# Matmuls of zeros in the planned pauses of TensorE, in a two-layer network on one core

## The chip, the core and the metric

The kernel runs on one core of a Trainium2 chip. The core has five engines that run their own instruction streams side by side: TensorE (PE in the profile; its weight loads are shown as PEld), VectorE (DVE), ScalarE (ACT), GpSimd (POOL) and SyncE (SP, which here only issues transfers). Each engine executes its instructions in the order of its stream, and waits on semaphores for the others. The metric is the device time of one execution in microseconds.

## The reference

The input is x, 8 images of 384 channels by 32 x 32 points (1024 tokens each). Layer 0 is a Mamba block that runs over the tokens forwards and backwards, beside a 3x3 depthwise convolution. Layer 1 is causal attention with 6 heads and a feed-forward part. The piece that matters here is the scan of layer 0, for each direction:

```python
delta = jax.nn.softplus(jnp.einsum('blr,dr->bld', dt, dt_proj_w) + dt_proj_b)
A = -jnp.exp(A_log)
deltaA = jnp.exp(delta[..., None] * A)
deltaBu = (delta * u)[..., None] * Bm[:, :, None, :]

def step(h, inp):
    dA, dBu, c = inp
    h = dA * h + dBu
    return (h, jnp.einsum('bdn,bn->bd', h, c))
...
y = ys.transpose(1, 0, 2) + u * D_param
y = y * silu(z)
return jnp.einsum('bld,od->blo', y, out_proj_w)
```

The state h has 16 components for each of 384 channels. The output y sums over these components, and in the kernel over both directions too.

## The kernel before

**Scans.** For every image, 96 groups are computed: each holds 8 channels x 16 state components on the 128 partitions and 1024 tokens along the free side, for one direction. The steps of a group (function `group`, within `scans`) are:

- SP loads delta, broadcast over the state components, into a tile dA; ACT takes the exponential with scale nA (L1007).
- PE spreads delta times u over the partitions with two matmuls by the 0/1 matrix dup (function `spread`; the profile calls its tile ring). The ring is 3 banks of PSUM; a group uses the middle bank and one of the two at the sides, so a spread into the middle bank has to wait until the scan before has read it.
- DVE multiplies both halves by B (L1035) and runs the scan over 1024 tokens (L1041), which reads two banks of the ring.
- POOL multiplies the result by C (L1045).

**Sums.** After every two groups PE adds them into the tile y with the 0/1 matrix sel (function `sums`). y is one bank of PSUM, [128, 512] in f32. Eight calls of `sums` (2 directions x GJ, GJ = 4) make one y: the first overwrites (start), the last ends the sum. Then DVE reads y (L983) and the next y takes over the same bank. There are 6 y for each image, 48 in all.

**Everything else.** Projections, convolutions, attention and feed-forward of the images around run in between, with four more banks of PSUM for their results. Nearly all matmuls are issued by the helper `mm` (L327), the transposes of attention by L1261. An f32 matmul appears as two MATMUL records and two weight loads.

**The order.** The program doesn't issue instructions as its loops run. Each step is entered as an `Op` with an engine, a cost in microseconds (functions act, dve, pool, pe, pair, quad at the top of the file), its reads, writes and due time. `Plan.run` plays the engines through with these costs: at each turn it takes the earliest operation that can start, with the waits for banks and transfers as it reckons them, and returns the operations sorted by their planned start. At the end of the kernel a loop emits them in that order, with `manual_schedule`, so that the order on each engine is the plan's, while the real waits are done by semaphores. A planned pause of PE is where the plan lets PE start an operation later than it ended the one before. The plan's pauses leave no instruction behind: on the chip PE simply waits for the semaphores of its next instruction.

Constants are made at the start of the kernel, among them ident, the 128 x 128 unit matrix in f32.

Of the kernel before, what the change touches and what calls it, by code (L numbers as in the profile page):

```python
# [9 lines left out]
F32 = mybir.dt.float32  # L10
# [7 lines left out]
P = 128  # L18
# [9 lines left out]
GJ = 4  # L28
# [37 lines left out]
class Val:  # L66


    __slots__ = ("kind", "shape", "dtype", "name", "t", "slot", "writes", "reads", "left", "end", "first")
# [4 lines left out]


class Op:
    __slots__ = ("engine", "cost", "fn", "vals", "allocs", "at", "waits", "users", "ready", "table", "done", "nbytes", "index", "after", "placed", "urgent")


def act(n):  # L80
# [24 lines left out]
class Plan:  # L105
# [63 lines left out]
    def run(self):  # L169

        engines = ("PE", "ACT", "DVE", "POOL", "SP")
        free = {e: 0.0 for e in engines}
        ready = {e: [] for e in engines}
        dma = 0.0
        table = None
        slots = {k: [(0.0, i) for i in range(n)] for k, n in self.slots.items()}

        queue = {k: [] for k in slots}
        for o in self.ops:
            for v in o.allocs:  # L180
                if v.kind != "psm":
                    queue[v.kind].append((o.at, o.index, v))
                    o.waits += 1
        for q in queue.values():
            q.sort(key=lambda a: a[:2])
            q.reverse()
        owner = {}
        for o in self.ops:
            for v in o.allocs:
                owner[id(v)] = o  # L190

        def release(o, t):
            o.ready = max(o.ready, t)
            o.waits -= 1
            if o.waits == 0:
                ready[o.engine].append(o)

        def hand_out(kind):
            while queue[kind] and slots[kind]:
                v = queue[kind].pop()[2]  # L200
                t, v.slot = heapq.heappop(slots[kind])
                release(owner[id(v)], t)

        for o in self.ops:
            if o.waits == 0:
                ready[o.engine].append(o)
        for kind in queue:
            hand_out(kind)
        order = []

        def bank_time(o):

            need = {}
            for v in o.allocs:
                if v.kind == "psm":
                    need[v.kind] = need.get(v.kind, 0) + 1
            t = 0.0
            for k, n in need.items():
                if len(slots[k]) < n:
                    return None  # L220
                t = max(t, sorted(slots[k])[n - 1][0])
            return t

        total = len(self.ops)
        while len(order) < total:
            best = None
            for e in engines:
                cand = []
                for o in ready[e]:
                    t = o.ready  # L230
                    if o.allocs:
                        tb = bank_time(o)
                        if tb is None:
                            continue
                        t = max(t, tb)
                    if e == "SP" and not o.urgent:
                        t = max(t, dma - self.BACKLOG)
                    cand.append((max(t, free[e]), o))
                if not cand:
                    continue  # L240
                t0 = min(c[0] for c in cand)

                pick, key = None, None
                for t, o in cand:
                    if t <= t0 + 0.05:
                        a = o.at - (self.STAY if e == "ACT" and o.table in (None, table) else 0.0)
                        k = (a, o.index)
                        if key is None or k < key:
                            pick, key, start = o, k, t
                if best is None or start < best[0]:  # L250
                    best = (start, e, pick)
            assert best is not None, "the slots do not suffice"
            start, e, o = best
            ready[e].remove(o)
            for v in o.allocs:
                if v.kind == "psm":
                    _, v.slot = heapq.heappop(slots[v.kind])
            cost = o.cost
            if e == "ACT" and o.table is not None and o.table != table:
                cost += self.SWITCH  # L260
                table = o.table
            free[e] = start + cost
            o.done = start + cost + self.LATENCY
            if e == "SP":
                dma = max(dma, start + cost) + o.nbytes / self.DMA_RATE
                o.done = dma + self.DMA_LATENCY + self.LANDING
            order.append((start, len(order), o))
            for u in o.after:
                release(u, start)
            for u in o.users:  # L270
                release(u, (o.done if u.engine != e or e == "SP" else free[e]) + (0.0 if u.urgent or u.engine == e else self.SLACK))
            for v in o.vals:
                v.left -= 1
                v.end = max(v.end, o.done)
                if v.left == 0 and v.kind is not None:
                    heapq.heappush(slots[v.kind], (v.end, v.slot))
                    if v.kind != "psm":
                        hand_out(v.kind)
        order.sort(key=lambda a: a[:2])
        return [o for _, _, o in order]  # L280
# [3 lines left out]
def conv_attn_hybrid_kernel(  # L284
# [20 lines left out]
    nc = tc.nc  # L305
    const = ctx.enter_context(tc.tile_pool(name="const", bufs=1))
# [4 lines left out]
    ident = const.tile([P, P], F32, name="ident")  # L311
# [14 lines left out]
    def mm(out_, lhsT, rhs, first=True, last=True):  # L326
        return nc.tensor.matmul(out_, lhsT=lhsT, rhs=rhs, start=first, stop=last)  # L327
# [1120 lines left out]
            forward(b, x2)  # L1448

    order = plan.run()  # L1450
    table = None
    with tc.manual_schedule():
        for o in order:
            for v in o.allocs:
                if v.kind in ("bs", "bm"):
                    continue
                p = pp if v.kind in ("psm", "y") else sb
                v.t = p.tile(v.shape, v.dtype, tag=f"{v.kind}_{v.slot}", name=v.name)
            if o.table is not None and o.table != table:
                table = o.table  # L1460
                nc.scalar.preload_act_table_set(table)  # L1461
            o.fn()


# [60 lines left out]
```

## Time and profile before

| What | Value |
|---|---|
| median of 3 runs | 4113.69 us (4110.54 to 4115.77) |
| the profiled execution, its own time | 4114.34 us |
| its span, from first to last instruction | 4112.4 us |
| mean granted clock of TensorE | 0.926 of full speed |
| scans on DVE (L1041) | 768, 2286 ns each, 1755.5 us |
| products by B on DVE (L1035) | 1536, 697 ns each, 1071.2 us |
| products by C on POOL (L1045) | 768, 2365 ns each, 1810.6 us |
| spreads on PE (ring) | 1536, 318.6 us busy |
| sums into y on PE | 3072 records, 533.5 us busy |
| idle of PE before a spread, until a scan ends | 339.0 us in 376 waits, at most 4.2 us |

In the profile, busy time is given for each engine, and also by 40 equal slices of the span, one digit for tenths of a slice. The row PEclk is the clock that TensorE was granted, in the same tenths. Matmuls are pipelined and their ends are modelled, so a busy PE isn't at its peak. The chain of waits follows the work that ended last back to what released it. A count such as x1536 is of instructions, and "128x512 f32" is partitions x elements.

### The profile page before, as it was taken

The page shows a single profiled execution, that of the slowest core. Times are in us where ns is not written, and L with a number is a line of the kernel's source. Part 1 is how long each engine was busy: PE and PEld are TensorE (multiplying, and loading weights), DVE is VectorE, ACT ScalarE, POOL GpSimd, SP SyncE. Part 2 cuts the span into 40 slices and gives each one's busy share as a digit, 9 for nine tenths or more (in the row PEclk, how much of TensorE's full clock was granted, in tenths as well). Part 3 has the DMA queues.
Part 4 walks back from the last instruction along what each step waited for, and adds up shares of the span by engine and source line. Part 5 has one row for each costly group of instructions (what it writes and reads, how often), then busy time and mean ns, then how long its engine had stood idle before and what let it go on. Part 6 is the DMA issues. An engine that isn't in the chain of part 4 may idle for free. (4 is left out here: it accounts for less than half of the span.)

```text
span 4112.4 us, 54637 instructions
## 1 busy us (share of the span) xinstructions
PE 3511.7 (85%) x17970; PEld 1407.7 (34%) x17970; DVE 3430.8 (83%) x3661; ACT 2815.4 (68%) x4547; POOL 3000.8 (73%) x2370
## 2 busy tenths in 40 slices
PE   6466658899998999898998899988999888898898
PEld 2111112443234422443234432444234432443363
DVE  2399989989989899888989899889998899999522
ACT  3766447775787758885778857786787766665364
POOL 1889786997589955997579965998479965775231
PEclk9687679899999999899999999999998899999999
DMA  7899897579976898669976798669975697559100
GB/s 243 233 258 275 254 263 203 156 227 256 265 207 181 233 265 242 189 207 240 271 211 196 218 260 248 197 199 246 253 230 174 177 255 203 141 161 228 48 9 35
DMA packets 302003, 858.96 MB, mean 209 GB/s; under 512 B 38312, under 2 KB 91576, under 8 KB 301720
## 3 DMA queue, kind: packets, MB, share of 16 engines
q1 hardware_dynamic: 301720, 855.47, 74.6%
q8 instruction: 143, 2.34, 0.2%
q14 instruction: 140, 1.15, 0.1%
HBM read 696.44 MB, written 160.68 MB: 208 GB/s over the span
## 5 line engine op out<-in xcount | busy, mean ns | idle before, releaser
L1045 POOL TENSOR_TENSOR dA<-dA,bc 128x1024 f32<-128x1024 f32 x768 | 1810.6, 2365 | 724.5 <-DVE dA L1041 638.7
L1041 DVE TENSOR_TENSOR_SCAN dA<-dA,ring 128x1024 f32<-128x1024 f32 x768 | 1755.5, 2286 | 91.4 <-ACT dA L1007 27.6
L1035 DVE TENSOR_TENSOR ring<-ring,bc 128x512 f32<-128x512 f32 x1536 | 1071.2, 697 | 286.1 <-PE ring L327 171.8
L1007 ACT ACTIVATE dA<-dA,nA 128x1024 f32<-128x1024 f32 x768 | 860.8, 1145 | 249.8 <-DMA dA<-ded 245.1
L327 PE MATMUL ring<-du,dup 32*128 32x512 bf16 x1536 | 318.6, 410 | 384.4 <-DVE dA L1041 339.0
L327 PE MATMUL y<-dA,sel 128*32 128x512 f32 x3072 | 533.5, 659 | 28.6 <-POOL dA L1045 26.2
L1208 ACT ACTIVATE p<-s,mx 128x512 f32<-128x512 f32 (+3 forms) x576 | 330.9, 581 | 99.7 <-DVE mx L1201 98.8
L1201 DVE TENSOR_REDUCE mx<-s 128x1 f32<-128x512 f32 (+3 forms) x576 | 286.0, 546 | 134.1 <-PE s L327 130.4
L1254 POOL TENSOR_SCALAR p<-p,den 128x512 f32<-128x512 f32 (+3 forms) x576 | 329.1, 590 | 79.0 <-issue 47.0
L327 PEld LDWEIGHTS <-dup 32*128 32x128 bf16 x1536 | 73.1, 92 | 887.1 <-DVE dA L1041 779.9
L1268 ACT COPY pT<-t 128x512 f32<-128x512 f32 (+3 forms) x576 | 258.1, 483 | 163.1 <-PE t L1261 156.2
L1261 PE MATMUL t<-ident,p 128*128 128x128 f32 x1728 | 298.1, 304 | 74.3 <-ACT pT L1268 26.2
L327 PE MATMUL s<-k,q 64*128 64x512 f32 (+3 forms) x1152 | 301.8, 571 | 20.6 <-ACT p L1208 19.1
L327 PE MATMUL pi<-xp,win 128*128 128x512 f32 x576 | 287.7, 621 | 3.5 <-DMA win<-in_in_wT 2.0
L1261 PEld LDWEIGHTS t<-ident,p 128*128 128x128 f32 x1728 | 206.1, 152 | 212.1 <-POOL p L1254 83.7
L1461 ACT ACT_TABLE_LOAD x210 | 269.4, 1283 | 4.5 <-PEq L1514 0.8
L327 PE MATMUL pc<-pT,v 128*64 128x128 f32 x3456 | 261.9, 294 | 10.1 <-ACT pT L1268 5.6
L327 PEld LDWEIGHTS pc<-pT,v 128*64 128x64 f32 x3456 | 204.4, 146 | 105.6 <-ACT pT L1268 38.6
L918 ACT CAST part<-u 128x1024 bf16<-128x1024 f32 x144 | 150.3, 1044 | 88.7 <-POOL u L926 49.1
L926 POOL TENSOR_TENSOR u<-u,part 128x1024 f32<-128x1024 f32 x96 | 205.0, 2135 | 5.6 <-ACT part L918 5.5
L327 PEld LDWEIGHTS y<-dA,sel 128*32 128x32 f32 x3072 | 82.3, 113 | 287.2 <-issue 137.9
L327 PEld LDWEIGHTS s<-k,q 64*128 64x128 f32 x1152 | 116.7, 197 | 144.4 <-ACT p L1208 64.4
(183 smaller groups left out, 4714.5 us busy)
## 6 DMA issues: line engine op xcount, KB each, us to landing
dA<-ded SPq DMA_DIRECT2D x768, 512.0 KB
ct<-urd SPq DMA_DIRECT2D x96, 513.5 KB
du<-dusd SPq DMA_DIRECT2D x96, 512.0 KB
xs<-xpd SPq DMA_DIRECT2D x96, 432.8 KB
dusd<-part SPq DMA_DIRECT2D x288, 128.0 KB
ded<-de SPq DMA_DIRECT2D x48, 512.0 KB
uz<-uzd SPq DMA_DIRECT2D x48, 512.0 KB
bc<-bcd SPq DMA_DIRECT2D x32, 512.0 KB
```

The lines of the kernel that those rows point to most:

```text
L327: return nc.tensor.matmul(out_, lhsT=lhsT, rhs=rhs, start=first, stop=last)
L926: "POOL", pool(L), lambda part=part: nc.gpsimd.tensor_sub(du.t, du.t, part.t), [part], [du]
L1007: "ACT", act(L) + 0.1, lambda: nc.scalar.activation(dA.t, dA.t, AF.Exp, scale=nA.t[:, g : g + 1]),
L1035: uses("DVE", nc.vector.tensor_mul(to, to, bc.t[:, 0, half(hf)]), [bank_of(v)])
L1041: i = nc.vector.tensor_tensor_scan(dA.t[:, rev], dA.t[:, rev], t[:, rev], 0.0, ALU.mult, ALU.add)
L1045: op("POOL", pool(L), lambda: nc.gpsimd.tensor_mul(dA.t, dA.t, bc.t[:, 1]), [(bc, 1)], [dA], at=at - PRODUCTS)
L1201: lambda sc=sc, g=g, w=k1 - k0, hh=hh: nc.vector.tensor_reduce(mx.t[:, g, hh : hh + 1], sc[hh].t[:, 0:w], AX.X, ALU.max, negate=True), [sc ...
L1208: nc.scalar.activation(ps[hh].t[:, k0:k1], sc[hh].t[:, 0 : k1 - k0], AF.Exp, bias=mx.t[:, g, hh : hh + 1], accum_out=den.t[:, g, hh : hh + 1],
L1254: nc.gpsimd.tensor_scalar(t, t, den.t[:, g, hh : hh + 1], 1.0, ALU.mult, ALU.mult)
L1261: nc.tensor.transpose(t.t[:, j * P - k0 : (j + 1) * P - k0], ps[hh].t[:, j * P : (j + 1) * P], ident)
L1268: nc.scalar.copy(pT[hh].t[:, k0 // P : k1 // P, :].rearrange("p j t -> p (j t)"), t.t[:, 0 : k1 - k0])
L1461: nc.scalar.preload_act_table_set(table)
```

## The change

After the plan has been made, the new code goes through the operations of PE in their order. Where the planned start of an operation lies more than 0.4 us after the planned end of PE's work so far, and a y has had at least one of its eight sums but not the last, it notes a number of pads for this operation: the pause less 0.2 us, divided by 0.25 us, rounded down. When the operations are emitted, so many matmuls of a 128 x 128 tile of zeros by ident are issued just before that operation. They are added onto the first 128 columns of the open y, without start and stop, so they add zero to it. The tile of zeros is written once, on POOL. The planner itself only stores each operation's start; costs, due times and order are untouched.

```diff
 class Op:
-    __slots__ = (..., "after", "placed", "urgent")
+    __slots__ = (..., "after", "placed", "urgent", "start")
...
+            o.start = start
             order.append((start, len(order), o))
...
     order = plan.run()
+
+    BUSY, REST = 0.25, 0.2
+    zeros = const.tile([P, P], F32, name="zeros")
+    nc.gpsimd.memset(zeros, 0.0)
+    at_work, parts_of, pads = 0.0, {}, {}
+    opened = None
+    for o in order:
+        if o.engine != "PE":
+            continue
+        pause = o.start - at_work
+        if opened is not None and pause > 2 * REST:
+            pads[id(o)] = (opened, int((pause - REST) / BUSY))
+        at_work = max(at_work, o.start + o.cost)
+        for v in o.vals:
+            if v.kind == "y":
+                parts_of[id(v)] = parts_of.get(id(v), 0) + 1
+                opened = v if parts_of[id(v)] < 2 * GJ else None
+
     table = None
     with tc.manual_schedule():
         for o in order:
...
+            if id(o) in pads:
+                y, k = pads[id(o)]
+                for _ in range(k):
+                    mm(y.t[:, 0:P], zeros, ident, False, False)
             o.fn()
```

## The prediction

> **What bounds the kernel now.** I read the page's engine totals and 40 slices first, then busy times by stretch, then waits, then the chain.
>
> ```profile
> PE 3511.7 (85%) x17970; PEld 1407.7 (34%) x17970; DVE 3430.8 (83%) x3661; ACT 2815.4 (68%) x4547; POOL 3000.8 (73%) x2370
> ...
> PE   6466658899998999898998899988999888898898
> DVE  2399989989989899888989899889998899999522
> ...
> POOL 1889786997589955997579965998479965775231
> PEclk9687679899999999899999999999998899999999
> ```
>
> PE, DVE and POOL share the bound. From slice 7 to slice 37 (617 to 3804 us, "the middle" below) PE is 91% and DVE 92% busy. From 206 to 617 us ("the head"; the scans of image 0 run, PE has little else) DVE alone sets the pace. After 3804 us ("the tail") there are no scans. How the pace looks where DVE sets it, from the chain of waits (start, length, what):
>
> ```profile
> 2906.39 2.30 DVE dA L1041
> 2910.39 2.30 DVE dA L1041
> 2914.39 2.30 DVE dA L1041
> ```
>
> One scan each 4.00 us: 2.29 of scan, two ring multiplies of 0.70, and 0.31 of handing over. So a DVE that waits for nothing still shows about 8% idle (0.31/4.00). In the attention stretches POOL is full as well (columns: stretch, length, busy us of PE, PEld, DVE, ACT and POOL with counts, clock, DMA share, GB/s):
>
> ```profile
> 3187.00:3290.00 103.00, 88.17 (x539) 44.50 (x533) 85.45 (x104) 76.20 (x163) 100.59 (x99) 0.88 0.61 177
> ```
>
> **The clock.** I asked for the busy times again in stretches of 3.413 us over the whole span. Nearly every stretch then shows a clock of 0.50 or 1.00, so it changes at these borders. One drop:
>
> ```profile
> 2211.82:2215.23 3.41, 2.95 (x20) 1.22 (x18) 3.20 (x3) 3.02 (x8) 3.35 (x3) 1.00 0.58 137
> 2215.23:2218.64 3.41, 1.57 (x8) 0.80 (x8) 3.31 (x8) 3.41 (x9) 3.31 (x3) 0.98 0.02 8
> 2218.64:2222.06 3.42, 0.86 (x4) 0.86 (x5) 3.42 (x6) 1.95 (x7) 3.42 (x6) 0.50 0.35 145
> 2222.06:2225.47 3.41, 3.41 (x19) 2.31 (x19) 2.25 (x3) 1.91 (x4) 3.27 (x5) 0.52 0.36 108
> 2225.47:2228.88 3.41, 3.16 (x39) 2.09 (x36) 3.09 (x6) 3.29 (x9) 2.62 (x5) 1.00 0.38 147
> ```
>
> PE is busy 46% of the second stretch; the next two run at half clock; a full stretch brings the clock back. In the middle all 19 warm stretches under 50% busy are followed by half clock, 8 of 27 at 50 to 60%, 11 of 131 at 60 to 80%, 1 of 673 above. There are 84 half-clock stretches there (287 us) in 39 episodes, 60 in the head (205 us), 8 in the tail.
>
> [...] The commonest kind (35 of some 78 us of idle in front of the drops) is the spread into the ring that waits for a scan:
>
> ```profile
> 1666.86 0.28 PE L327 MATMUL s<-neg,ident 128*128 128x128 bf16 x2
> 1668.47 0.39 PE L327 MATMUL ring<-du,dup 32*128 32x512 bf16 x2 [1.32 <-DVE dA L1041]
> ```
>
> **What the change adds.** Nothing is removed or moved: the planner's order is as before (the new field only stores a start). One memset on POOL at the start lies beside the first 100 us, in which POOL works 14. Then pads: a 128x128 f32 product of zeros each, ahead of a PE operation whose planned start leaves over 0.4 us of pause, while a y is between its first and eighth sum.
>
> Price of one pad. The nearest row is the v projection, the same shape and type; with its start and length and that of a 512-column f32 sum from the chain:
>
> ```profile
> 3964.32 5.36 PE pvv L327 x48
> ...
> 4055.64 5.15 PE pv_f L327 x12
> ```
>
> An f32 product is two MATMUL records (1152 pvv records for 576 products), so a pad is 5.36/24 = 0.223 us warm, about 0.446 at half clock; the plan allows 0.25. [...] I take the row, which is f32.
>
> Number of pads. The plan's pauses are no view of the profile, so I bound them by the real ones. PE gaps over 0.4 us: 68 in the head (143 us) and 322 in the middle (287 us); the rule of the diff, int((gap - 0.2)/0.25), makes 474 and 735 of them. y is open for about 7/8 of the time: 415 and 640. The plan counts 0.967 us for a 512-column f32 product where the trace has 5.15/6 = 0.86, so it sees less pause; against that it counts 1.07 for a sum into y where 533.5/384 = 1.39 are busy. I take 415 + 500, about 900 pads; ends 500 (few pauses planned) and 1500 (DVE's plan slower than I think). [...]
>
> What hides them: the very wait that the pause foresees. PE executes in order, so a pad costs only where PE reaches that place late. Behind it then stand the spread, the ring multiply, the scan and its POOL product. A pad runs 0.027 us shorter than allowed, 0.2 us and on average 0.12 of rounding stay free, and the plan's DVE has no handing over (3.69 us a scan against 4.00), so real waits at a scan should be longer than planned ones. If the cover is gone for all 500 pads of the middle: +111 us. If it holds: 0. I take one pad in eight uncovered, 14 us of PE, of which a fifth reaches DVE (it waits for PE in only part of the middle): +3 us.
>
> In the head a step leaves PE idle for 3.6 us in every 4.0 where it has nothing else:
>
> ```profile
> 238.93:242.34 3.41, 0.61 (x2) 0.10 (x2) 3.07 (x4) 1.15 (x1) 3.41 (x3) 0.50 0.78 265
> ```
>
> 13 pads are 2.9 us warm, inside the gap; the first such gap may meet the half clock (5.8 us) and hold DVE for 2.4 us, once or twice.
>
> What a steady clock is worth. Upper end: PE is busy 259 us in the middle's half-clock stretches; at full clock that work takes half, 130 us less, if PE alone were the path. Lower end: 0, if POOL and DVE cover all. The nearest rows are the waits of DVE in the middle (us, times, longest):
>
> ```profile
> DVE ring L1035 <- PE ring L327: 63.2, 70, 3.0
> DVE mx L1201 <- PE s L327: 38.5, 33, 4.2
> ```
>
> DVE's busy share is 0.847 in the half-clock stretches, 0.813 in the first stretch after each, 0.917 in the other warm ones. So the half clock costs DVE (0.917-0.847)x287 = 20 us and (0.917-0.813)x137 = 14 us, 34 together, a third of the 102 us of the two waits. The head adds (0.927-0.889)x205 = 8. I take three quarters of the 42 as prevented, because nearly all drops begin with y open, but those begun by a late POOL or DMA are foreseen only in part: -31 us. The tail has no open y: 0.
>
> Sum: 4114.3 (the profiled execution: 4112.4 of span and 2 around it) - 31 + 3 = 4086. It stands 0.6 us from the median of the runs, 4113.7, so 4086 against that too. What is late next is DVE with its 4.00 us a scan, and POOL in attention.
>
> **Rivals.**
> 1. *The pads take PE's room to catch up* (slower). PE's idle is also its slack after a late DMA or POOL. Filled with a fixed count, it no longer absorbs them, and pads run while a spread is due. The place is the ring spread in the attention stretches; the price 0.223 us a pad. It decides from 31/0.223 = 140 uncovered pads on the path. At half of the 500: +56 - 31, 4139. For it: the order is fixed and PE 91% busy. Against: the margins above.
> 2. *Hidden anyway* (no change). The drops lie mostly in attention, where POOL is at 97 to 99%; a faster PE waits for it. Then only the head's few us are left, 4108 to 4114. Against: the 63 and 38 us that DVE waits for PE.
> 3. *The pads don't do it* (no change): few planned pauses fall on the drops, or products of zeros don't count as work for the clock. No row shows zeros. 4114.
> 4. *PE is the path in the middle* (more). Three quarters of the 130 us are won: 4114 - 97 = 4017. For it: backlog from a half-clock episode lasts beyond the one stretch that I counted. Against: DVE is just as full.
>
> **How the numbers follow.** This kernel's runs lie within 0.13%, so 0.2% (8 us) is what can be told from no change: 4105.5 to 4122. Forecast (4065 to 4105) 0.53; rival 4 0.14; rivals 2 and 3 together 0.14; rival 1 0.19. Faster: 0.53 + 0.14 = 0.67; same 0.14; slower 0.19. The range takes the forecast's and both same-cases, reaches down over most of rival 4, and up to about its half-way mark in rival 1: 4030 to 4135.
>
> **What would show it.** Right: some 1800 more PE MATMUL records at y from zeros; the mean clock from 0.926 to about 0.96, the head's digits at 8 or 9; in the middle fewer than 30 half-clock stretches; PE's wait for scans down from 339 us to under 150; DVE's wait for PE below 63. Wrong: a clock that stays (rival 3), a clock that rises with the same span (2), DVE's wait for the spread above 63 us (1), or a span under 4050 (4).

## The result and the profile after

| | before | with the change |
|---|---|---|
| median of 20 runs each | 4116.65 us | 4110.17 us |
| ratio, 95% interval | | 0.9980 (0.9968 to 0.9992) |
| mean clock of TensorE in the profile | 0.926 | 0.964 |
| half-clock stretches (3.4 us) in the head / the middle | 60 / 84 | 10 / 37 |
| PE busy in the profile | 3511.7 us | 3650.7 us |

The change gains 0.2%, some 8 us, where 28 were forecast. The clock did what was expected of it as a mean: 0.96 was forecast. In the middle 37 half-clock stretches are left, where fewer than 30 were forecast. The page of the changed kernel, its totals and slices:

```profile
PE 3650.7 (89%) x20072; PEld 1623.8 (39%) x20072; DVE 3431.1 (83%) x3661; ACT 2815.7 (68%) x4547; POOL 3001.4 (73%) x2371
...
PE   6478889899998989889988989889998989998998
...
PEclk9699999999999999999999999999999999999899
...
L328 PE MATMUL ring<-du,dup 32*128 32x512 bf16 x1536 | 307.1, 393 | 307.7 <-DVE dA L1042 265.0 <-DMA du<-dusd 32.1 <-DVE den L1248 4.9
...
L328 PE MATMUL y<-ident,zeros 128*128 128x128 f32 x2102 | 296.2, 287 | 0.0
```

The head is slices 3 to 6: there the digits of PE went from 5 or 6 to 7 or 8, those of the clock from 6 to 8 up to 9. PE's idle before the spreads, until a scan ends, fell from 339 us only to 265.0; under 150 was named as the sign of being right. Most of the pads' time did not go into that wait. The last row is the pads: 2102 records, two to a pad, so 1051 pads (900 forecast), about 500 of them in the middle (500 forecast). DVE's waits for PE in the middle, the rows that answer to 63.2 and 38.5 before:

```profile
DVE ring L1036 <- PE ring L328: 48.0, 64, 2.4
DVE mx L1202 <- PE s L328: 32.1, 29, 4.2
```

They fell by 22 us. Yet the profiled execution before took 4112.4 us of span and this one 4113.8. Single runs scatter by more than the effect (4103 to 4126 with the change), so I took a second profile of each kernel:

> The kernel before once more, for a second profile. If the first was typical: 75 to 95 half-clock stretches in the middle, DVE waits 95 to 115 us for PE there, of which some 50 in or just after half clock.

> The changed kernel once more, for a second profile. If the first was typical: 30 to 45 half-clock stretches in the middle, DVE waits 75 to 95 us for PE there, of which under 25 in or just after half clock, and 50 to 65 where PE is warm and full.

The spans were 4122.8 and 4104.4. In the middle there were 89 and 40 half-clock stretches, DVE waited 111.1 and 79.9 us for PE, 57.2 and 25.3 of it in or just after half clock (the second a little over the 25 expected), and 51.7 with the change where PE was warm and full. Both first profiles were typical.

**A way to add up.** From the last read of y of image 0 to that of image 7, DVE has the same work in every kernel that keeps its work. I summed its idle gaps there, by what ended them (gaps between two instructions of one kind are left out). The time of this stretch less the idle is 3021 to 3026 us in all of these profiles, so what differs between kernels in this stretch is DVE's idle:

| profile | stretch, us | DVE idle | ended by PE | by ACT, POOL, DMA |
|---|---|---|---|---|
| before, two profiles | 3274.1, 3279.3 | 250.0, 256.5 | 109.2, 115.4 | 46.1, 46.5 |
| change, two profiles | 3277.6, 3267.4 | 253.7, 243.6 | 102.8, 98.8 | 56.1, 49.0 |

The rest of the idle, 94 to 96 us in each of the four, is short gaps between DVE's own instructions, and the change leaves it as it is. Means: DVE's idle falls by 4.6 us. Inside it:

- waits for PE that end in half clock or in the 3.4 us after it, in the middle: 51.5 and 57.2 before, 24.9 and 25.3 after, **-29 us**. This is the gain the change is after.
- waits for PE where it is warm and was over 90% busy in the 6 us before: 47.4 and 46.1 before, 53.5 and 51.7 after, **+6 us**. Those where it was warm but had been idle: -3. (With the limit at 95% these two are +2 and 0.)
- waits for PE between image 0 and 617 us: 0.7 and 0.8 before, 6.5 and 6.6 after, **+6 us**.
- waits for PE after 3804 us, the last 40 us of the scans: 3.0 and 3.8 before, 12.9 and 12.4 after, **+9 us**.
- waits for ACT, POOL and transfers: **+6 us**, with 7 between the two profiles of the change. Probably a DVE that is earlier meets the others sooner; that is not shown.

The head gives another -3 (image 0 ends at 569.6 and 572.2 before, 568.4 and 568.0 after). Together about -8, which is what was measured. With two profiles of each kernel, 10 us apart, the terms of 3 to 6 us are known only roughly, but for the +6 before 617 us: it is a single block of pads, the same in both profiles of the change. PE's order, and DVE's wait in that place:

```profile
605.06 7.63 PE L328 MATMUL y<-ident,zeros 128*128 128x128 f32 x66
612.63 0.39 PE L328 MATMUL ring<-du,dup 32*128 32x512 bf16 x2
```

```profile
DVE ring L1036 <- PE ring L328: 6.1, 1, 6.1
```

The plan has a pause of over 8 us there (33 pads at 0.25), and 33 pads were put into it. Before, PE waited 3.2 to 3.6 us for a scan ahead of the spreads around that time. The spread comes late and DVE stands for 6.1 us.

The +6 of the middle has no single place. What can make it, in the order of PE's work with the change (start, length, what, idle before and what ended it):

```profile
789.21 0.61 PE L328 MATMUL y<-ident,zeros 128*128 128x128 f32 x4
790.72 0.39 PE L328 MATMUL ring<-du,dup 32*128 32x512 bf16 x2 [0.90 <-DVE dA L1042]
791.03 1.16 PE L328 MATMUL y<-ident,zeros 128*128 128x128 f32 x8
792.12 1.06 PE L328 MATMUL y<-dA,sel 128*32 128x512 f32 x8
793.12 0.49 PE L328 MATMUL y<-ident,zeros 128*128 128x128 f32 x2
793.46 0.93 PE L1262 MATMUL t<-ident,p 128*128 128x128 f32 x4
```

The first two pads lie in a real wait: after them PE still waits 0.90 us for a scan. The next four and the one after do not: the sum and the transposes follow at once, so they were ready before the pads ended, and the pads made them late by up to their whole length. Counted over the middle, 371 of 498 pads are followed by work without any idle: 149 of them stand ahead of sums into y, 77 ahead of scores, 67 of transposes, and only 17 ahead of spreads. The plan lets these operations start later than they are ready on the chip. Which of its costs is too long there is not shown.

The +9 at the end of the scans is one place too, the same in both profiles of the change. PE's order and the busy times (PE, PEld, DVE, ACT, POOL, then the clock) there:

```profile
3819.10 1.65 PE L328 MATMUL y<-ident,zeros 128*128 128x128 f32 x6
3820.68 2.08 PE L328 MATMUL ph<-fy,w_fc 32*128 32x512 f32 x4
3822.68 1.94 PE L328 MATMUL y<-dA,sel 128*32 128x512 f32 x8
3824.55 0.61 PE L328 MATMUL ring<-du,dup 32*128 32x512 bf16 x2
```

```profile
3816.00:3820.00 4.00, 4.00 (x10) 2.07 (x11) 3.04 (x4) 1.78 (x3) 2.35 (x1) 0.50 0.00 0
3820.00:3824.00 4.00, 4.00 (x16) 1.16 (x15) 2.60 (x2) 1.09 (x2) 1.93 (x1) 0.50 0.00 0
3824.00:3828.00 4.00, 4.00 (x18) 0.81 (x14) 2.70 (x2) 0.00 (x0) 0.43 (x1) 0.50 0.00 0
```

PE is full and stays at half clock for 34 us. Three pads take 1.65 us there, where they took 0.94 at full clock just before, and the spread is due before it is issued: DVE waits 2.5 us for it. That the clock stayed at half through these 34 us, with PE full, is not what the prediction had assumed.

### The profile page after: what moved, and what is told of

Same layout as the page of the kernel before. It is cut to its first block, busy times and chain, and to the rows that moved or that the text cites. A ratio compares the mean times of both kernels' runs of the same rounds, so it can differ in the third digit from the quotient of the medians.

```text
span 4113.8 us, 58842 instructions
## 1 busy us (share of the span) xinstructions
PE 3650.7 (89%) x20072; PEld 1623.8 (39%) x20072; DVE 3431.1 (83%) x3661; ACT 2815.7 (68%) x4547; POOL 3001.4 (73%) x2371
## 5 line engine op out<-in xcount | busy, mean ns | idle before, releaser
L328 PE MATMUL ring<-du,dup 32*128 32x512 bf16 x1536 | 307.1, 393 | 307.7 <-DVE dA L1042 265.0
L328 PE MATMUL y<-dA,sel 128*32 128x512 f32 x3072 | 474.6, 619 | 13.0 <-POOL dA L1046 6.8
L1269 ACT COPY pT<-t 128x512 f32<-128x512 f32 (+3 forms) x576 | 256.5, 484 | 150.1 <-PE t L1262 143.3
L1262 PE MATMUL t<-ident,p 128*128 128x128 f32 x1728 | 283.4, 292 | 54.3 <-POOL p L1255 23.8
L328 PE MATMUL y<-ident,zeros 128*128 128x128 f32 x2102 | 296.2, 287 | 0.0
L328 PE MATMUL s<-k,q 64*128 64x512 f32 (+3 forms) x1152 | 278.2, 546 | 12.5 <-ACT p L1209 11.1
L328 PEld LDWEIGHTS y<-ident,zeros 128*128 128x128 f32 x2102 | 258.3, 195 | 69.8 <-issue 69.8
L1262 PEld LDWEIGHTS t<-ident,p 128*128 128x128 f32 x1728 | 195.2, 146 | 178.4 <-POOL p L1255 80.2
L328 PE MATMUL pc<-pT,v 128*64 128x128 f32 x3456 | 248.0, 284 | 4.7 <-ACT pT L1269 4.1
L328 PEld LDWEIGHTS pc<-pT,v 128*64 128x64 f32 x3456 | 192.6, 139 | 91.5 <-ACT pT L1269 35.4
```

The costliest lines, as they stand in the source:

```text
L1262: nc.tensor.transpose(t.t[:, j * P - k0 : (j + 1) * P - k0], ps[hh].t[:, j * P : (j + 1) * P], ident)
L1269: nc.scalar.copy(pT[hh].t[:, k0 // P : k1 // P, :].rearrange("p j t -> p (j t)"), t.t[:, 0 : k1 - k0])
```

## The experiments

Ratios are to the kernel before, with 95% intervals. "Half-clock stretches" and "waits" are those of the middle.

**e1, pads where PE was seen idle.** The pads' places and numbers come from the trace of before, ahead of spreads only:

```diff
-        pause = o.start - at_work
-        if opened is not None and pause > 2 * REST:
-            pads[id(o)] = (opened, int((pause - REST) / BUSY))
+        if any(v.kind in ("bs", "bm") for v in o.vals):
+            if opened is not None and nth in SEEN:
+                pads[id(o)] = (opened, SEEN[nth])
+            nth += 1
```

> Pads not where the plan has pauses but where the trace of before shows PE idle over 0.4 us ahead of a spread into the ring (259 gaps, 1023 pads by the same formula, those outside an open y skipped). Theory A (what was won is hidden: DVE's 4.00 us a scan and POOL set the end, PE does not): the clock rises to 0.95 or more, the time is as with the change, ratio 0.996 to 1.000. Theory B (the clock is worth some 30 us, and pads that run where PE is late give 20 us of it back): here nearly all pads lie in real idle, so the ratio is 0.991 to 0.995.

Measured 0.9988 (0.9977 to 1.0000), clock 0.951: both in theory A's ranges, and theory B's is missed. It is no proof of A, since the mean clock rose mostly in the head. Of some 290 pads in the middle 240 had idle left behind them, and the waits with PE warm and full were 50.5 us, between those before (47) and with the change (53). But 66 half-clock stretches remained there, with 41.6 us of waiting. Covered pads cost little, and these held the clock little too. Neither theory had that.

**e2, e3: PE lighter and heavier.**

```diff
 def sums(...):
+    if j == 1:
+        return
```

> The changed kernel without the sums of j = 1 (96 of 384 calls; a quarter of the terms of y is left out), which takes 474.6/384 = 1.24 us each, about 119 us, from PE, some 95 us of them in the middle. Theory A: at most 15 us of it reach the end, ratio 0.994 to 0.998. Theory B (PE on the path in the middle): 30 to 95 us reach it, ratio 0.975 to 0.991.

Measured 0.9983 (0.9970 to 0.9996), the same as with the change, just over theory A's range and far from theory B's. As a test of PE's place it fell short: half-clock stretches went up from 37 to 55, so that PE was busy only 46 us less in the middle, not 95. What was taken from PE's work came back with the clock (0.955 on average, against 0.964).

```diff
             o.fn()
+            for v in o.vals:
+                if o.engine == "PE" and v.kind == "y":
+                    sums_of[id(v)] = sums_of.get(id(v), 0) + 1
+                    for _ in range(2 if sums_of[id(v)] < 2 * GJ else 0):
+                        mm(v.t[:, 0:P], zeros, ident, False, False)
```

> The changed kernel with 2 more pads after each of the first seven sums of every y, whether PE has a pause or not: 672 more pads, 150 us of PE at 0.223 each, about 125 us in the middle. Theory A: PE's room takes it up, ratio up to 1.001. Theory B (uncovered pads cost about a quarter of their length): 30 us or more above the change, ratio 1.005 to 1.012.

Measured 1.0100 (1.0073 to 1.0127): 42 us above before, 50 above the change, for 672 more pads at an equal clock (33 half-clock stretches). That is a third of the pads' 150 us. DVE's waits for the spread answer directly (48.0 with the change):

```profile
DVE ring L1036 <- PE ring L328: 98.2, 113, 7.2
```

So pads that run where PE is late do reach the end, at about 0.07 us each. That is theory B, at a third of their length instead of the quarter it named.

**e4, e12, e13: which part of the kernel.** Pads only after image 0, not in the last y, and both:

```diff
-        if opened is not None and pause > 2 * REST:
+        if opened is not None and pause > 2 * REST and len(parts_of) > 6:            # e4
+        if opened is not None and pause > 2 * REST and len(parts_of) < 6 * B:        # e12
+        if opened is not None and pause > 2 * REST and 6 < len(parts_of) < 6 * B:    # e13
```

> The changed kernel with the pads of image 0 (514 of them) left out, those of the middle kept. Theory A: ratio 0.997 to 1.000. Theory B: the same, 0.997 to 1.000, unless the pads in the head cost time (DVE waited once 6.1 us for a spread there), then 0.995 to 0.997.

> The changed kernel without the pads of the last y. In both profiles of the change PE runs at half clock, full, through the last 35 us of the scans, and DVE waits 14 us more for it there than before. If the pads of that stretch cause it: DVE's waits for PE in the last 45 us of the scans fall under 6 us, ratio 0.994 to 0.997. If it is the place where the clock happened to drop: the waits stay over 10 us, ratio 0.996 to 0.999.

> Pads neither in image 0 nor in the last y. A candidate for the best version: ratio 0.994 to 0.997 if the end of the scans cost the change something, 0.996 to 0.999 if not.

Measured 0.9970 (0.9952 to 0.9987), 0.9973 (0.9961 to 0.9985) and 0.9973 (0.9960 to 0.9986). The 514 pads of image 0 bring nothing that can be measured, though they lift its clock from 0.75 to 0.96: DVE sets the pace there. In e12 and e13 DVE waits for PE about 4 us in the last 50 us of the scans, against 13 in both profiles of the change. But e4 keeps its pads there and shows no stall either (3.8 us), so the pads alone don't make it; in both profiles of the change the half clock falls just there. What it is worth in the median can't be told apart from nothing: e12's and e13's ratios lie where the expectations put an end of the scans that cost the change little (0.996 to 0.999).

**e5, e6: DVE and POOL lighter.**

```diff
             def times_b(v=v):
+                if j == 1 and r == 0:
+                    return
```

> The changed kernel without DVE's products by B of one group in eight (j = 1, r = 0: 192 of 1536 products, 134 us; those states are left unweighted). Theory C (DVE's own work sets the end, and what PE wins is lost in it): 80 us or more of the 134 reach the end, ratio 0.965 to 0.980. Theory D (PE, DVE and POOL are each near the end, none alone): at most 40 us, ratio 0.988 to 0.997.

```diff
+        def times_c():
+            if j == 1 and r == 0 and d == 0:
+                return
+            nc.gpsimd.tensor_mul(dA.t, dA.t, bc.t[:, 1])
```

> The changed kernel without POOL's product by C of one forward group in eight (48 of 768, 2.367 us each, 114 us; those states go unweighted into y). Theory C: at most 15 us reach the end, ratio 0.994 to 0.999. Theory D: 15 to 40 us, ratio 0.988 to 0.994. If POOL were the bound: 80 us or more, ratio under 0.98.

Measured 0.9890 (0.9861 to 0.9918) and 0.9960 (0.9947 to 0.9973). Against the change's 0.998 that is 37 us of DVE's 134 and 8 of POOL's 114. DVE's idle rose to 339.6 us in e5, 165.2 of it ended by PE (101 with the change): PE takes over. Theory D holds for DVE: it is near the end, and PE is right behind it. For POOL the 8 us are what theory C had named.

**e7 to e10: which pads.** e7 places pads in all gaps seen, not only ahead of spreads (by a list of places as in e1, not shown here); e8 keeps the change's pads ahead of spreads and transposes, e9 all others, e10 those after image 0 in planned pauses over 1.0 us.

```diff
+        due = any(v.kind in ("bs", "bm") or v.kind == "psm" and v.name.startswith("t_") for v in o.vals)
-        if opened is not None and pause > 2 * REST:
+        if opened is not None and pause > 2 * REST and due:        # e8; "and not due" in e9
```

> Pads in all gaps of PE over 0.4 us that the trace of before shows, ahead of whatever operation stands there, if y is open (246 gaps, 862 pads). If the gain is limited by what the pads cost where PE is late (12 us more of DVE waiting in full stretches with the change), it goes away here: DVE's waits for PE in the middle fall from 106 us to under 75, half-clock stretches there to 40 or fewer, ratio 0.994 to 0.997. If the end is held elsewhere, the same waits fall and the ratio stays at 0.997 to 0.999.

> The changed kernel with its pads kept only ahead of spreads and of attention's transposes, where about half found PE really waiting; those ahead of sums, scores and the rest, nearly all of them late, are dropped. If late pads take back part of the gain: ratio 0.994 to 0.997. If they cost nothing: 0.997 to 0.999.

> The complement of e8: the changed kernel with its pads kept ahead of sums, scores and everything else but spreads and transposes; nearly all of these run where PE is late. Theory E (late pads only cost; the clock is held by those in real pauses): ratio 1.000 to 1.005, half-clock stretches in the middle over 60. Theory F (late pads hold the clock too, since they take up the wait that would come next): ratio 0.996 to 0.999, 35 to 55 half-clock stretches.

> The changed kernel with pads only after image 0 and only where the plan's pause is over 1.0 us, the pauses that can pull a stretch of 3.4 us under the busy share that drops the clock; the short ones go. Theory E: the price falls more than the gain, ratio 0.993 to 0.997. Theory F: part of the clock's gain is lost, ratio 0.997 to 1.000.

| | ratio | half-clock stretches | DVE's waits for PE |
|---|---|---|---|
| e7 | 0.9976 (0.9965 to 0.9986) | 58 | 93.3 us |
| e8 | 1.0002 (0.9987 to 1.0016) | 65 | 109.1 us |
| e9 | 1.0005 (0.9991 to 1.0018) | 60 | 104.2 us |
| e10 | 0.9987 (0.9970 to 1.0004) | 54 | 105.2 us |

None of the four is better than the whole set beyond its interval; each half of it alone (e8, e9) gains nothing. e8 missed both its ranges, and e7 the waits and stretches that it named. e9's ratio lies in theory E's range, e10's in theory F's. Dropping late pads did not help, and keeping late pads alone neither. The number of pads doesn't settle it: e7 has some 470 in the middle, nearly as many as the change, and 58 half-clock stretches to its 37.

**e11: what does the clock go with?** Half-clock stretches that are full of work are not alike: the clock comes back after some and not after others. "Rows" and "columns" below are the two numbers that stand first in a product's form in the profile, as 32 and 128 in 32*128. One in the tail of the kernel before, PE's order and its busy times:

```profile
4079.14 1.92 PE L327 MATMUL pz<-g,w_p 128*32 128x512 f32 x4
4080.99 2.08 PE L327 MATMUL ph<-fy,w_fc 32*128 32x512 f32 x4
```

```profile
4078.89:4082.31 3.42, 3.42 (x10) 0.69 (x8) 0.00 (x0) 1.08 (x2) 0.00 (x0) 0.50 0.00 0
4082.31:4085.72 3.41, 3.41 (x8) 0.69 (x8) 0.00 (x0) 1.67 (x3) 0.00 (x0) 0.50 0.02 5
```

PE is 100% busy and the clock stays at half (0.50 in both), while after the full stretch shown in the prediction (2222.06 to 2225.47), one of mostly 128-row products (transposes), it was 1.00. Here half of the time is pz, 128 rows and 32 columns, and half is ph, 32 rows and 128 columns. In the fourteen profiles taken up to e10, in half-clock stretches with PE over 93% busy, I added up what filled them by what came next, in stretches (clock comes back, clock stays): ph, 32 rows, 5.7 and 56.9; pd, 24 rows, 0.5 and 30.0; transposes, 128 rows, 94.4 and 19.9; sums into y, 128 rows and 32 columns, 121.8 and 21.9. Hence the test:

```diff
-                    mm(y.t[:, 0:P], zeros, ident, False, False)
+                    mm(y.t[:, 0:P], zeros[0:KI, :], ident[0:KI, :], False, False)
```

> The changed kernel with the same pads, but of 32 rows instead of 128 (zeros[0:32] by ident[0:32]): the same length on PE, a quarter of the array's rows. In the traces, half-clock stretches that are full of 32-row products (ph) or 24-row ones (pd) do not bring the clock back, those full of 128-row ones do. If rows count: the clock stays near 0.93, 75 or more half-clock stretches in the middle, and only the price of the pads is left, ratio 1.000 to 1.006. If busy time alone counts: as the change, clock 0.96, 30 to 45 stretches, ratio 0.996 to 0.999.

Measured 1.0232 (1.0207 to 1.0257), 96 us slower, clock 0.918, 93 half-clock stretches: the clock is what "rows count" had named, the price is far above its 1.000 to 1.006. With the same pads at the same places, on a quarter of the rows, the clock was not held:

```profile
PE   6489999999998999989898999989998998999998
...
PEclk9677585999998999999998999989998999999999
...
L328 PE MATMUL y<-ident,zeros 32*128 32x128 f32 x2102 | 393.6, 350 | 0.0
```

PE is 92% busy in the head, and the clock there is lower than in the kernel before (0.71 against 0.75). In this run the clock went with the rows and not with busy time. And it shows the pads' price without the gain: +55 us in the head (image 0 ends at 625.1 us), +36 us in the scans after it (3313.0 us against 3276.7). It is an upper end, since pads at half clock take longer: in the profile of the change the starts of a pad's two records lie 213 ns apart there (median), and 112 at full clock. A record takes 350 ns on average in e11, 287 with the change.

A pad of 32 rows also has a quarter of the rows times columns, so both changed together. The traces tell them apart. In all nineteen profiles I cut the time from 200 us on at the clock's own borders, and in each stretch weighted PE's busy time by rows: each product's time, from its start to the next one's, by its rows as a share of 128. At half clock, all 332 stretches with 90% or more of this weighted time were followed by full clock, and none of the 499 with under 50%. At full clock, 2 of 17483 with 60% or more were followed by a drop, and 267 of 274 with under 30%. Busy time alone sorts worse: with PE 90% busy or more the clock came back after 693 of 1104. So does weighting by rows times columns: at half clock 265 of the 1102 stretches under 50% came back. In the stall at the end of the scans nine stretches, with PE at 100%, had 59 to 73% by rows, and the clock stayed at half; the tenth had 100%, and the clock came back.

**e14, e15: rows without pads.** The spreads are 32-row products and there are 1536 of them. Taken over all rows, with zeros in dup, they compute the same:

```diff
+    dup4 = const.tile([P, P // KI, P], BF16, name="dup4")
+    nc.gpsimd.memset(dup4, 0.0)
+    for q in range(P // KI):
+        nc.vector.tensor_copy(dup4[q * KI : (q + 1) * KI, q], dup[q * KI : (q + 1) * KI])
...
-                rr = slice((r * NH + hf) * KI, (r * NH + hf + 1) * KI)
-                uses("PE", mm(to, dup[rr, :], du3.t[rr, j]), [bank_of(v)])
+                uses("PE", mm(to, dup4[:, r * NH + hf], du3.t[:, j]), [bank_of(v)])
```

> The kernel before, no pads, with each spread taken over all 128 rows (dup with the other rows zeroed, four such matrices, by the whole du3), so that the 1536 spreads, which are 32-row products, count in full for the clock if rows count. The two spreads of a group, 0.39 us together when they ran side by side on different rows, now run one after the other, some 0.6 us: 768 times 0.2, 154 us more of PE. If rows count: fewer than 60 half-clock stretches in the middle (84 and 89 before). Time: at the price of e3 (42 us for 150 us of PE) against the gain of e11 (some 40 us in the middle), ratio 0.995 to 1.005; if the spreads' real waits hide the longer spread, 0.988 to 0.995.

Measured **0.9942 (0.9921 to 0.9963)**, in the range for spreads that are hidden by real waits. It is clearly better than the change (0.9980), and lower than every version with pads alone, though the intervals of e4, e12 and e13 overlap with its own. The spread and DVE's two waits for PE:

```profile
1659.85 0.60 PE L327 MATMUL ring<-du,dup 128*128 128x512 bf16 x2 [0.74 <-DVE dA L1045]
```

```profile
DVE ring L1039 <- PE ring L327: 38.0, 61, 1.4
DVE mx L1205 <- PE s L327: 33.5, 28, 4.2
```

A pair takes 0.60 us where it took 0.39: its two products start 226 ns apart, where they had started 3 ns apart, side by side on different rows. DVE still waits less, 38.0 for 63.2. Half-clock stretches are 39, as with the change, and no late pad is paid for. From image 0 to the end of the scans DVE is idle 230.8 us, 79.9 of it ended by PE. The mirror image, e14 with the change's pads on top:

> e14's spreads over all rows, with the pads of the change as well. If the pads' gain is the clock and their price is PE's time: the clock is held already (39 half-clock stretches in the middle with e14, as with the change), so little gain is left and the price of some 30 us in the middle comes on top, ratio 0.997 to 1.003, worse than e14's 0.994. If the two add up: 0.990 to 0.993.

Measured 0.9966 (0.9953 to 0.9979), just under the range for a price without a gain. The clock is higher still (24 half-clock stretches, 0.975), the time is not lower than e14's; the intervals overlap a little. With the clock held by other means no gain of the pads is left that shows.

## Why the prediction was wrong

- **What bounds the kernel**: right. DVE is busy some nine tenths of the scans in every profile, and PE is the largest single cause of its idle. (The 91 and 92% for PE and DVE in the middle are 89.4 and 90.8; nothing hangs on it.)
- **The clock by 3.4 us stretches**: right as a record of what happens, including its drops in stretches of low busy share. In the first profiles of the two kernels all but the last of the 118 and 54 spells of one clock last a whole number of 3.41 us. Most of the 39 drops of the middle came after single gaps of 1.3 to 2.4 us, and the longest that begins there is 3.2 us, at 624. Incomplete in its cause: it took PE's busy share for what the clock goes with, and a full stretch for one that brings it back. After half-clock stretches with PE 90% busy or more the clock came back in 693 of 1104; after those with 90% or more by rows, in all 332. In e11, with PE 92% busy in the head, it was 0.71 there.
- **Number and length of pads**: right for the middle, where 500 were taken and 498 are in the trace; in the head there are more than the 415 taken. A record lasts 287 ns, and the next starts 112 ns after it began (median, full clock), so a pad takes the 0.223 us that was reckoned.
- **The gain**: about right. In the middle three quarters of 34 us, some 26, were taken, and the waits in and after half clock fell by 29. The head was to give some 6 and gave 3.
- **The cover of the pads**: this is the step that failed. "I take one pad in eight uncovered, 14 us of PE, of which a fifth reaches DVE": +3 us. In the trace three in four (371 of 498) have no idle behind them, up to 83 us of PE at 0.223 each, and in e3 a third of such time reached the end. By that rate it is up to 28 us. In the waits of the two pairs of profiles it is some 21: +6 in the middle, +6 from the one block at 605 us, +9 at the end of the scans, where the half clock has its part. The reason given, that real waits for scans are longer than planned, holds for most of the pads ahead of spreads, but not for the block at 605 us. And the plan's pauses mostly stand ahead of sums, scores and transposes, which are ready early on the chip.
- **What is late next**: DVE and POOL were named, and put at nothing. DVE waits 6 us more for ACT, POOL and transfers.
- **Rivals**: the first, the pads taking PE's room, had the mechanism. Its place was right only in part (sums and scores more than the spread), and its turning point of 140 uncovered pads on the path wasn't reached: 21 us are as much as 94. The time lies in the second rival's range of 4108 to 4114, but not for its reason: the waits for PE in the middle did fall, by 27 us, and the head's few us, which it left standing, don't show in e4. The third was wrong, since the clock rose. The fourth was wrong too: the clock rose and 8 us came of it.

The sum as the runs have it: -29 in the middle's half clock, -3 in the head, -3 in other waits, +6, +6 and +9 from late pads and the half clock at the end, +6 from the others: -8. Not settled is the exact share of the pads in the +9, since e4, with the same pads there, doesn't show it, and why covered pads (e1, e7) hold the clock less well than the plan's.

## What to carry to other kernels

Work that is added to fill a planned pause costs wherever the pause isn't there; check in the trace whether idle is left behind it, not only whether there is idle on average. Before adding work to keep a clock up, look in the trace at what fills the busy stretches after which it stays low (here 32-row and 24-row products: 56.9 and 30.0 stretches of ph and pd after which it stayed, 5.7 and 0.5 after which it came back), and widen those that are there anyway: e14 did so with the spreads, and was the faster kernel (0.9942, against 0.9980 with pads). Loading an engine and lightening it are different questions: 150 us more on PE cost 50 us (e3), while taking sums away from it gained nothing that could be measured (e2): its clock fell with them, from 0.964 to 0.955.

## What the runs showed of the hardware

These are measurements of this kernel and its variants; why the clock goes as it does is not shown.

- In the nineteen profiles the clock sorted by PE's busy time weighted by rows: at half clock all 332 stretches with 90% or more were followed by full clock, and none of 499 with under 50%; at full clock 2 of 17483 with 60% or more were followed by a drop, and 267 of 274 with under 30%. Busy time alone (back after 693 of 1104 with 90% or more) and rows times columns (back after 265 of 1102 with under 50%) sorted worse.
- With pads of 128 rows the head's clock was 0.96, against 0.75 before; with the same pads of 32 rows, and PE 92% busy there, it was 0.71. At the end of the scans, with the change, nine stretches in a row had PE 100% busy and 59 to 73% by rows, and were at half clock, over 30 us together; the tenth had 100% by rows, and full clock followed.
- The pads are products of zeros by the unit matrix, and the clock of 0.96 in the head was reached with them.
- The two spreads of a group, on different blocks of 32 rows, started 3 ns apart (0.39 us for both); on all rows they started 226 ns apart (0.60 us). The kernel with the longer form was the faster one (0.9942).
